# Sixteen expert blocks computed at the end of the first stage instead of at the start of the second

## The chip, the cores and the metric

One core of one Trainium2 chip runs the whole program. The core has TensorE (PE, with its weight loads shown apart as PEld), VectorE (DVE), ScalarE (ACT), GpSimd (POOL) and SyncE (SP, which here only issues DMAs). The metric is the device time in microseconds (us) of one execution; shown is the median of several runs. All engines take their instructions in order, each from its own queue, and wait for each other by semaphores.

## The reference

The input x has 32 sequences of 56 rows of 256 numbers; ctx has 32 x 1500 rows of 256. All is float32. Four layers follow each other, each with a residual:

```
x = x + xattn0(layernorm(x), ctx)   # decayed sum over ctx, projected, one vector per sequence; layernorm
x = x + ffn0(layernorm(x))          # 16 experts of width 176, the best 6 of each row
x = x + xattn1(layernorm(x), ctx)   # masked softmax attention over the 1500 rows
x = x + ffn1(layernorm(x))          # 2 experts of width 1024, the best one of each row

# ffn0, h: (1792, 256)
scores = softmax(h @ gate_w.T); topk_w, topk_idx = top_k(scores, 6)
y = sum over e of  cw[:, e] * ((silu(h @ w_gate[e].T) * (h @ w_up[e].T)) @ w_down[e].T)
```

Here only ffn0 matters, and the stage ahead of it that decides which rows go to which expert.

## The kernel before, in words

**Stages.** The kernel has four stages: a loop over 16 pairs of sequences (the first stage: context sum, first residual, normalised rows, choice of experts, sorting), the blocks of ffn0 (the second stage), attention, and the blocks of ffn1. Constants: P = 128, NP = 16 pairs, E0 = 16 experts, K0 = 6, F0 = 176, H0 = 88, NB0 = 95 blocks.

**First stage (lines 643 to 767).** Each step p of the loop streams two sequences' context through `ring`, five slots of SBUF (`count_in`, L315), and works at the same time on the pairs before: `first_norm`, `residual`, `second_root`, `second_norm` (L491, the normalised rows xn), `away` (L497, xn to the DRAM table `xn0`), `turned` and `gate` (the gating product), `best` (L511, the six best experts of each row, `sel`), `ranks` (L528, how many rows of each expert lie before), `counted` and `places` (L534, L540, each row's place in its expert's list and its level, that is the block of 128 in the list), `ones_at` (L566, one-hot rows, some experts' on DVE and some on POOL) and `sorted_in` (L588, matmuls that add to `owned` in PSUM: for each expert, level and place the row's number and its weight). `base0` counts the rows of each expert so far. In the last steps the weights of ffn0 are loaded into `w0_sb` (`load_w0_up`, L209; `w0_down_pieces`, L217, issued by `some_pieces`).

**The tail (lines 685 to 767).** After the loop come the last pair's steps, one after the other: norm, gate, `best(last)`, `ranks(last)`, `counted(last)`; then the table of blocks is made from the counts (`real`, `slot`, `blk`, `hot`), `owned` is copied out (L746), and eight matmuls (L750) turn it into `idx` (for each of the 95 blocks the numbers of its 128 rows), `wgt` (their weights) and `ei` (the place of the block's expert in `w0_sb`). Blocks are ordered by level: blocks 0 to 15 are the first 128 rows of the 16 experts, if each has any row. `busy(n)` (L579) runs n filler matmuls on PE.

**Second stage (`expert_blocks`, L769).** For each block: `rows_of` (L941) gathers its 128 rows from `xn0` by an indirect DMA on POOL's queue, seven blocks ahead; PE turns them (L195) and ACT copies them (L197); `gate_up` (L778) multiplies by gate and up weights (L785), ACT applies Silu (L791), DVE multiplies (L797); PE turns the product (L803), DVE copies it (L805), `down` multiplies (L812), ACT copies the result (L951) and SP writes it to the DRAM table `ys0` (L952). PE runs gate of block t, turn of t-1, rows of t+1 and down of t-2 in one step t. `side(t)` (L1039) does other work in each step: `ways_` (where each row's six results lie), windows of the context for the attention (`load_window`, one per step from step 1 to 16), a copy of xr to DRAM (step 17), mask rows, zero rows, and from step 20 on gathers of results (`result`, L853, POOL) that DVE adds to the rows (L1032).

**What sets the order.** Under `manual_schedule` an engine's instructions stay in the order in which the program writes them; this holds for PE, DVE, ACT and SP in the whole kernel, and for POOL too from the second stage on. In the first stage POOL's order is chosen by the framework's scheduler. SP issues transfers in program order. ACT needs its table of functions exchanged between logarithm/exponential and Silu. If `bad` is set at the end (some assumption on the data doesn't hold), a general path computes everything from ffn0 on again.

Of the kernel before, what the change touches and what calls it, by code (L numbers as in the profile page):

```python
# [19 lines left out]
P = 128  # L20
# [23 lines left out]
NB0 = NBW - E0 // 4  # L44
NY1 = 3
NB1 = B * S // P + 1
WP = 2 * D + 2
# [12 lines left out]
def xattn_ffn_kernel(  # L60
# [91 lines left out]
    starts = const.tile([1, B], I32, name="starts")  # L152
    bad = const.tile([1, 1], I32, name="bad")

    ring = const.tile([P, NRING, CW], F32, name="ring")
# [52 lines left out]

    def load_w0_up():  # L209
        for m, w in ((0, wg0), (1, wu0)):  # L210
            for k in range(KD):
                nc.sync.dma_start(
                    out=w0_sb[:, :, (2 * k + m) * F0 : (2 * k + m + 1) * F0],
                    in_=w[:, k, :].rearrange("p (e f) -> p e f", f=F0),
                )
# [18 lines left out]
    with tc.tile_pool(name="p1", bufs=1) as p1, tc.tile_pool(name="p3", bufs=3) as p3, tc.tile_pool(  # L234
# [151 lines left out]
        for l in range(NL):  # L386
            G.memset(lev[:, l, :], float(l * P))
        iota = p1.tile([P, P], F32, name="iota")
# [107 lines left out]
        def away(p):  # L496
            nc.sync.dma_start(out=xn0[p * P : (p + 1) * P, :], in_=pend[p]["xn"])  # L497
# [80 lines left out]

        def busy(n):  # L579

            for _ in range(n):
                d = psa.tile([P, 512], F32, tag="acc", name="d")
                PE.matmul(
                    d, lhsT=ident, rhs=slots[B % NRING][:, 0:2, :].rearrange("p j d -> p (j d)"),
                    start=True, stop=True,
                )

        def sorted_in(p, h=None):  # L588

            t = pend[p]  # L590
            for e in range(E0) if h is None else range(NE * h, NE * h + NE):
                c, g = divmod(e, 4)
                PE.matmul(  # L593
                    owned[Q * g : Q * g + Q, c, :],
                    lhsT=vals[:, p % 2, e].rearrange("p o l -> p (o l)"),
                    rhs=t["hots"][e // NE][:, e % NE, :],
                    start=(p == 0 and c == 0), stop=(p == NP - 1 and c == 3),
                )
# [42 lines left out]


        for p in range(NP):
            if p >= 1:
                first_norm(p - 1)
# [9 lines left out]
            if p >= 2:  # L655
                ranks(p - 2)
            sum_in_columns(p)
            if p >= 3:
                ones_at(p - 3, 1)
            if p >= 1:  # L660
                second_norm(p - 1)
                away(p - 1)
                some_pieces(1)
            projected(p)
            if p >= 3:
                sorted_in(p - 3)
            if p >= 1:
                turned(p - 1)
# [12 lines left out]
            if p == NP - 3:  # L681
                load_w0_up()
            if p > NP - 3:
                some_pieces(6)
        last = NP - 1
        first_norm(last)
        ones_at(NP - 3, 0)
        residual(last)
        ones_at(NP - 3, 1)
        second_root(last)  # L690
        ranks(NP - 2)
        second_norm(last)
        away(last)
        some_pieces(len(pieces))
        sorted_in(NP - 3, 0)
        turned(last)
        sorted_in(NP - 3, 1)
        gate(last)
        busy(1)
        counted(NP - 2)  # L700
        places(NP - 2)
        best(last)
        ranks(last)
        for h in range(2):
            ones_at(NP - 2, h)
        for h in range(2):
            sorted_in(NP - 2, h)
        counted(last)


# [14 lines left out]
        for c in range(4):  # L725
# [4 lines left out]
            )  # L730
        busy(1)
        places(last)
        for h in range(2):
            ones_at(last, h)
        blk = p2.tile([P, 4], F32, name="blk")
        V.tensor_copy(blk, bp[:, 0:4])
        hot = slots[B % NRING].rearrange("p j d -> p (j d)")
        own, hot = hot[:, 0 : 4 * P].rearrange("p (c r) -> p c r", c=4), hot[:, 4 * P :]
        hot = hot[:, 0 : 8 * NB0].rearrange("p (c b) -> p c b", c=4)
        V.tensor_tensor(  # L740
            hot, i99.rearrange("p o b -> p (o b)").unsqueeze(1).to_broadcast([P, 4, 2 * NB0]),
            blk.unsqueeze(2).to_broadcast([P, 4, 2 * NB0]), ALU.is_equal,
        )
        for h in range(2):
            sorted_in(last, h)
        A.copy(own.rearrange("p c r -> p (c r)"), owned.rearrange("p c r -> p (c r)"))  # L746
        bl = ps.tile([P, 512], F32, tag="ps", name="bl")
# [15 lines left out]
        PE.transpose(ep[0:1, 0:P], ex, ident)  # L763
        busy(2)
        V.tensor_copy(idx, bl[:, 0:NB0])
        V.tensor_copy(wgt, bl[:, P : P + NB0])
        V.tensor_copy(ei, ep[0:1, 0:P])

    def expert_blocks(nb, nq, f, w, ei, wk, ptr, pgu, pht, py, rows_of, done, ahead, wgt=None, side=None, xT0=None):  # L769

# [3 lines left out]
        piece = doff + 2 * D  # L774
        units = [(i, u) for i in range(nb) for u in range(nq)]
        xT, at, hs, hT, y = {}, {}, {}, {}, {}
# [42 lines left out]

        xb = {i: rows_of(i) for i in range(min(ahead, nb))}  # L820
        xT[0] = xT0 or turned_rows(wk, ptr, "tr", xb[0])
        xb.pop(0)
        if side:
            side(-1)
        for t in range(len(units) + 2):
            if t < len(units):
                gate_up(*units[t])
            if 0 <= t - 1 < len(units):
                turn(*units[t - 1])
            if t < len(units) and units[t][1] == nq // 2 and units[t][0] + 1 < nb:  # L830
                i = units[t][0] + 1
                if i + ahead - 1 < nb:
                    xb[i + ahead - 1] = rows_of(i + ahead - 1)
                xT[i] = turned_rows(wk, ptr, "tr", xb.pop(i))
            if t >= 2:
                down(*units[t - 2])
            if side:
                side(t)

# [88 lines left out]
    with tc.manual_schedule(  # L928
# [8 lines left out]
        zrow = rt.tile([P, WP], F32, name="zrow")  # L937
        G.memset(zrow, 0.0)
        G.memset(zrow[:, WP - 1 : WP], float(FAR))

# [70 lines left out]
        def late_or_bad():  # L1011
# [7 lines left out]
            V.tensor_reduce(t8s[0:1, 0, 0:1], lp[0:1, 0:P], AX.X, ALU.max)  # L1019
            V.tensor_scalar(bad, t8s[0:1, 0, 0:1], 0.0, bad, ALU.is_gt, ALU.max)  # L1020
            V.tensor_scalar(
                bad, slot[0:1, NL - 1, E0 - 1 : E0], float(NB0), bad, ALU.is_gt, ALU.max
            )

        todo = [(blocks_by(p) + 4, p, k) for p in soon for k in range(K0)]
        sums = []
# [12 lines left out]
        def side(t):  # L1039
# [5 lines left out]
            if t > 1:  # L1045
                for _ in range(3):
                    if ways_:
                        next_ = ways_.pop(0)
                        next_()
            if 0 < t <= B // 2:  # L1050
                load_window(t - 1)
            if t == B // 2 + 1:
                nc.sync.dma_start(
                    out=xr0.rearrange("(p r) d -> r p d", r=P), in_=xr,
                )
            if 0 < t - B // 2 - 1 <= B:
                b = t - B // 2 - 2
# [33 lines left out]
            NB0, 1, F0, w0_sb.rearrange("p e w -> p (e w)"), ei,  # L1091
            wk, ptr, pgu, pht, py, rows_of, done, 7, wgt, side,
        )
# [590 lines left out]
```

## Time and profile before

| | us |
|---|---|
| median of 7 runs | 781.97 |
| lowest, highest | 778.65, 783.93 |
| the profiled execution | 783.53 |
| its span (first to last instruction) | 781.8 |
| PE busy in the span | 672.3 |
| DVE busy | 402.0 |
| POOL busy | 351.3 |
| ACT busy | 238.0 |
| mean granted clock of PE | 0.945 of full |

The profile is of one execution. Its durations are those of single instructions; "idle before" is the time in which an engine waited ahead of an instruction, and what follows the arrow is what released it. A granted clock below 1 means that PE ran slower than it could. The DMA share is the mean busy share of 16 DMA engines and can read slightly above 1.

### The profile page before, as it was taken

What the parts mean: (1) busy time and instruction counts of PE and PEld (TensorE: products, weight loads), DVE (VectorE), ACT (ScalarE), POOL (GpSimd) and SP (SyncE); (2) the same over time, 40 slices, a digit from 0 to 9 for tenths busy, and PEclk for the clock granted to TensorE, in tenths of its full rate; (3) what the DMA queues carried; (4) which work ended last, traced back from release to release, by engine and by line L of the source; (5) the groups of instructions that cost most, each with busy time, mean ns of one, the idle gap of its engine ahead of it and who ended that gap; (6) DMA issues with size and microseconds to landing.
All of it is one profiled execution on the core that took longest, in us unless ns stands there. A gap on an engine that the chain in (4) does not pass through costs nothing.

```text
span 781.8 us, 13508 instructions
## 1 busy us (share of the span) xinstructions
PE 672.3 (86%) x4099; PEld 442.6 (57%) x4099; DVE 402.0 (51%) x1378; ACT 238.0 (30%) x704; POOL 351.3 (45%) x440
## 2 busy tenths in 40 slices
PE   3468878887789988788899888899987999999996
PEld 3334545554557766566566656556653566666664
DVE  3568787788436535333344334668787332333232
ACT  0123333333124433233333323266653111111110
POOL 5355566643243465366665665546642411221210
PEclk9779999997689999899999999999999899999999
DMA  8959999998248976344444443377881200110100
GB/s 264 365 225 376 351 370 366 340 344 258 65 132 265 309 255 201 87 131 133 123 133 125 123 140 112 108 233 202 220 272 51 95 13 22 41 27 28 41 28 17
DMA packets 70656, 136.62 MB, mean 175 GB/s; under 512 B 7731, under 2 KB 43204, under 8 KB 70580
## 3 DMA queue, kind: packets, MB, share of 16 engines
q1 hardware_dynamic: 56036, 100.31, 37.4%
q0 software_dynamic: 14544, 35.37, 16.4%
q8 instruction: 38, 0.62, 0.3%
q14 instruction: 38, 0.31, 0.1%
HBM read 109.54 MB, written 26.77 MB: 174 GB/s over the span
## 4 chain that ended last, share of the span: by engine, by line
PE 76%; DVE 8%; ACT 4%; issue 3%; POOL 3%; DMA 2%; another core or an unknown queue 1%; SPq 1%; POOLq 0%; DVEq 0%; ACTq 0%
PE gu L785 28%; PE y L812 18%; PE acc L325 6%; PE tp L803 4%; PE tp L195 4%; PE tp L913 2%; DMA xr<-in_x 2%; PE op L1177 2%; PE sp L1142 2%; ACT xT L197 2%; PE bp L467 1%; PE owned L593 1%; POOL xn L491 1%; PE lp L505 1%
## 5 line engine op out<-in xcount | busy, mean ns | idle before, releaser
L785 PE MATMUL gu<-w_sb,xT 128*128 x380 | 137.9, 486 | 29.2 <-ACT xT L197 22.1
L943 POOL DMA_INDIRECT xb<-xn,idx x95 | 93.1, 980 | 100.1 <-PE tp L195 51.2
L791 ACT ACTIVATE sg<-gu 128x176 f32<-128x176 f32 (+1 forms) x155 | 53.1, 343 | 252.5 <-PE gu L785 218.3
L797 DVE SCALAR_TENSOR_TENSOR hs<-sg,wgt,gu 128x176 f32<-128x176 f32 x95 | 37.8, 397 | 153.5 <-ACT sg L791 130.3
L785 PE MATMUL gu<-ring,xT 128*128 x240 | 114.7, 601 | 0.5 <-issue 0.5
L785 PEld LDWEIGHTS gu<-w_sb,xT 128*128 128x128 f32 x380 | 71.7, 197 | 65.5 <-ACT xT L197 29.7
L812 PE MATMUL y<-w_sb,hT 88*128 x380 | 99.7, 385 | 0.8 <-ACT yb L951 0.8
L856 POOL DMA_INDIRECT g<-ys,early x78 | 74.2, 951 | 36.0 <-issue 16.8
L795 DVE TENSOR_TENSOR hs<-sg,gu 128x256 f32<-128x256 f32 x60 | 25.2, 420 | 114.2 <-ACT sg L791 112.6
L803 PEld LDWEIGHTS tp<-ident,hs 128*88 128x88 f32 (+1 forms) x310 | 40.7, 132 | 62.4 <-issue 50.8
L1428 POOL DMA_INDIRECT out<-ob,ti x15 | 14.8, 989 | 130.2 <-DVE ob L1425 129.9
L812 PEld LDWEIGHTS y<-w_sb,hT 88*128 88x128 f32 x380 | 65.7, 193 | 6.8 <-ACT yb L951 1.0
L805 DVE COPY hT<-tp 88x256 f32<-88x256 f32 (+1 forms) x155 | 64.4, 416 | 8.1 <-PE y L812 5.0
L197 ACT COPY xT<-tp 128x256 f32<-128x256 f32 x126 | 46.9, 372 | 62.7 <-PE tp L195 38.7
L785 PEld LDWEIGHTS gu<-ring,xT 128*128 128x128 f32 x240 | 45.8, 192 | 33.5 <-issue 30.7
L812 PE MATMUL y<-ring,hT 128*128 x240 | 62.6, 384 | 0.0
L803 PE MATMUL tp<-ident,hs 128*88 128x128 f32 (+1 forms) x310 | 60.8, 279 | 1.7 <-issue 1.5
L325 PE MATMUL acc<-ring,cz 128*32 128x256 f32 x768 | 55.4, 447 | 0.3 <-DVE cz L301 0.3
L951 ACT COPY yb<-y 128x256 f32<-128x256 f32 x95 | 35.6, 375 | 55.0 <-PE y L812 34.2
L432 POOL TENSOR_SCALAR z<-xr,mva,rsa 128x256 f32<-128x256 f32 x16 | 23.0, 1437 | 49.2 <-DVE xr L479 45.0
L195 PE MATMUL tp<-ident,xb 128*128 128x128 f32 x220 | 43.1, 279 | 0.8 <-issue 0.8
L812 PEld LDWEIGHTS y<-ring,hT 128*128 128x128 f32 x240 | 41.5, 193 | 3.4
(307 smaller groups left out, 997.7 us busy)
## 6 DMA issues: line engine op xcount, KB each, us to landing
ring<-in_cx SPq DMA_DIRECT2D x32, 1536.0 KB
ys<-yb SPq DMA_DIRECT2D x95, 128.0 KB
ring<-in_cx SPq DMA_DIRECT2D x16, 384.0 KB
extra<-in_cx SPq DMA_DIRECT2D x16, 384.0 KB
xs<-zrow SPq DMA_DIRECT2D x5, 771.0 KB
w_sb<-in_wg SPq DMA_DIRECT2D x2, 1408.0 KB
w_sb<-in_wu SPq DMA_DIRECT2D x2, 1408.0 KB
xn<-xn SPq DMA_DIRECT2D x16, 128.0 KB
```

The source lines that it names most:

```text
L195: PE.transpose(tp[:, k * P : (k + 1) * P], xn[:, k * P : (k + 1) * P], ident)
L197: A.copy(xT.rearrange("p k c -> p (k c)"), tp[:, 0 : KD * P])
L325: PE.matmul(acc[Q * g : Q * g + Q, 0:D], lhsT=cz[:, j, 1 - h : 1 - h + Q], rhs=c[:, j, :], start=(h == 0 and m == 0), stop=(h == 1 and m = ...
L785: PE.matmul(gu[:, 0 : 2 * fp], lhsT=xT[i][:, k, :], rhs=w[:, bass.ds(at[i] + (u * piece + k * 2 * fp), 2 * fp)], start=(k == 0), stop=(k = ...
L791: A.activation(sg, gu[:, 0:fp], AF.Silu)
L797: V.scalar_tensor_tensor(hs[i, u], sg, wgt[:, i : i + 1], up, ALU.mult, ALU.mult)
L803: PE.transpose(tp[0:h, c * P : (c + 1) * P], a[:, c * h : (c + 1) * h], ident)
L805: V.tensor_copy(hT[i, u], tp[0:h, 0 : 2 * P])
L812: PE.matmul(y[i][:, 0:D], lhsT=a[:, c * P : (c + 1) * P], rhs=w[0:h, bass.ds(at[i] + (u * piece + doff + c * D), D)], start=(u == 0 and c ...
L856: G.indirect_dma_start(out=g, out_offset=None, in_=ys0[0 : n * P, :], in_offset=bass.IndirectOffsetOnAxis(ap=at[:, p, k : k + 1], axis=0),)
L943: G.indirect_dma_start(out=xb, out_offset=None, in_=xn0, in_offset=bass.IndirectOffsetOnAxis(ap=idx[:, i : i + 1], axis=0),)
L951: A.copy(yb, y[:, 0:D])
```

## The change

The first 128 rows of each expert are taken from the first eight pairs alone. What `owned` holds after pair 7 is copied out (`first_copy`, in step 10), and level 0 of it gives the rows and weights of blocks 0 to 15 (`first_table`, in step 11: `idx0`, `wgt0`). Their gathers (`soon_rows`) and their matmuls (`soon_turned`, `soon_gate`, `soon_step`) stand in program order among the last pair's steps, and what is left of them after `idx` is there. They use the slots of `ring` that the context no longer needs, the PSUM pools of the first stage, and constant addresses of `w0_sb`. `sorted_in` starts `owned` anew at pair 8, and the saved part is added at the end (DVE in place of ACT's copy). `lack` sets `bad` if an expert had fewer than 128 rows by pair 7 and got more later. The second stage starts at block 16: `expert_blocks` gets `first`, windows are loaded two per step from step 16 to 23, the copy of xr comes in step 15, gathers of results no earlier than step 24. POOL is in fixed order from step 15 of the first stage on. `busy` is gone. Silu now is needed first in the tail, after `best(last)`, so that the function table changes there, once. `load_w0_up` is split by experts: 0 to 3 and 4 to 11 in step 13, 12 to 15 at the end of step 15, followed by all the pieces that are left.

The core of the diff:

```diff
+PC = 8
-            G.memset(lev[:, l, :], float(l * P))
+            G.memset(lev[:, l, :], float(l * P) if l else -1.0)
...
+        def first_copy():
+            V.tensor_scalar(cut, base0[0:1, :], float(P), None, ALU.min)
+            A.copy(own0, owned.rearrange("p c r -> p (c r)"))
...
+        def soon_rows(n):
+            for _ in range(n):
+                i = len(egot)
+                if i < E0:
+                    egot.append(i)
+                    G.indirect_dma_start(
+                        out=xbs[i], out_offset=None, in_=xn0[0 : PC * P, :],
+                        in_offset=bass.IndirectOffsetOnAxis(ap=idx0[:, i : i + 1], axis=0),
+                    )
...
+        def soon_turned(i):
+            tp = ps.tile([P, 512], F32, tag="ps", name="tp")
+            for k in range(KD):
+                PE.transpose(tp[:, k * P : (k + 1) * P], xbs[i][:, k * P : (k + 1) * P], ident)
+            exT[i] = two_of("xT", 0, D).rearrange("p (k c) -> p k c", k=KD)
+            A.copy(exT[i].rearrange("p k c -> p (k c)"), tp[:, 0:D])
...
+        def soon_step(copy=A.copy):
+            t = eat[0]
+            eat[0] += 1
+            if t < E0:
+                gu = egu.pop(t)
+                sg = two_of("sg", 2 * D, F0)
+                A.activation(sg, gu[:, 0:F0], AF.Silu)
+                hs = two_of("hs", 2 * D + F0, F0)
+                V.scalar_tensor_tensor(
+                    hs, sg, wgt0[:, t : t + 1], gu[:, F0 : 2 * F0], ALU.mult, ALU.mult
+                )
+                if 2 <= t + 1 < E0:
+                    soon_gate(t + 1)
+                tp = ps.tile([P, 512], F32, tag="ps", name="tp")
+                for c in range(2):
+                    PE.transpose(tp[0:H0, c * P : (c + 1) * P], hs[:, c * H0 : (c + 1) * H0], ident)
+                ehT[t] = two_of("hT", D, D)[0:H0]
+                copy(ehT[t], tp[0:H0, 0 : 2 * P])
+            if t + 2 < E0:
+                soon_turned(t + 2)
+            if t >= 1:
...
+                yb = ybs[i % 8]
+                A.copy(yb, y[:, 0:D])
+                nc.sync.dma_start(out=ys0[i * P : (i + 1) * P, :], in_=yb)
...
         for p in range(NP):
+            if p == NP - 1:
+                pool_too.enter_context(
+                    tc.manual_schedule(engines={ET.PE, ET.DVE, ET.Activation, ET.SP, ET.Pool})
+                )
...
                 away(p - 1)
+                if p == NP - 1:
+                    soon_rows(2)
...
             if p == NP - 3:
-                load_w0_up()
+                load_w0_up(0, 4)
+                load_w0_up(4, 12)
             if p > NP - 3:
                 some_pieces(6)
+            if p == NP - 1:
+                A.copy(own.rearrange("p c r -> p (c r)"), own0)
+                load_w0_up(12, E0)
+                some_pieces(len(pieces))
         last = NP - 1
+        soon_turned(0)
+        soon_turned(1)
+        soon_rows(1)
         first_norm(last)
         ones_at(NP - 3, 0)
         residual(last)
         ones_at(NP - 3, 1)
+        soon_rows(2)
         second_root(last)
         ranks(NP - 2)
+        soon_gate(0)
         second_norm(last)
         away(last)
-        some_pieces(len(pieces))
+        soon_rows(2)
         sorted_in(NP - 3, 0)
         turned(last)
         sorted_in(NP - 3, 1)
         gate(last)
-        busy(1)
+        soon_gate(1)
         counted(NP - 2)
         places(NP - 2)
         best(last)
+        soon_rows(3)
         ranks(last)
+        soon_step()
         for h in range(2):
             ones_at(NP - 2, h)
+        soon_rows(2)
+        soon_step()
         for h in range(2):
             sorted_in(NP - 2, h)
         counted(last)
...
-        busy(1)
+        soon_step()
+        soon_rows(4)
         places(last)
         for h in range(2):
             ones_at(last, h)
+            soon_step()
...
+        soon_step()
         for h in range(2):
             sorted_in(last, h)
-        A.copy(own.rearrange("p c r -> p (c r)"), owned.rearrange("p c r -> p (c r)"))
+        V.tensor_tensor(own, owned, own, ALU.add)
+        soon_step()
...
-        busy(2)
         V.tensor_copy(idx, bl[:, 0:NB0])
         V.tensor_copy(wgt, bl[:, P : P + NB0])
         V.tensor_copy(ei, ep[0:1, 0:P])
+        while eat[0] < E0 + 1:
+            soon_step(V.tensor_copy)
...
-            if 0 < t <= B // 2:
-                load_window(t - 1)
-            if t == B // 2 + 1:
+            if t == E0 - 1:
+                G.memset(zrow, 0.0)
+                G.memset(zrow[:, WP - 1 : WP], float(FAR))
                 nc.sync.dma_start(
                     out=xr0.rearrange("(p r) d -> r p d", r=P), in_=xr,
                 )
+            if 0 <= t - E0 < B // 4:
+                for h in range(2):
+                    load_window(2 * (t - E0) + h)
```

## The prediction

> **What bounds the kernel now.** I read the busy time by stretch first, then the timeline around the end of the first stage and the first steps of the second, then the waits there. Columns of the first view: stretch, its length, busy time of PE, PEld, DVE, ACT and POOL (with counts), granted clock, DMA share, GB/s.
>
> ```profile
> 176.00:185.00 9.00, 7.87 (x102) 4.82 (x101) 7.48 (x29) 3.25 (x12) 4.13 (x7) 1.00 1.14 337
> 185.00:213.60 28.60, 20.48 (x146) 13.45 (x146) 17.71 (x54) 5.30 (x16) 7.20 (x11) 0.64 0.38 108
> 213.60:260.00 46.40, 43.12 (x188) 30.95 (x189) 22.12 (x73) 16.92 (x47) 20.17 (x22) 0.93 0.69 204
> ```
>
> The loop over pairs ends near 185.0. From there to the first expert matmul at 213.6, the tail, a DVE chain (places, one-hots, block table) sets the pace; PE is busy 20.48 us of 28.6, but at a clock of 0.64. From 213.6 on PE sets it (43.12 of 46.4). So PE time is scarce behind 213.6 and partly free before. One step of the second stage in its steady state:
>
> ```profile
> 228.81 1.35 PE L785 MATMUL gu<-w_sb,xT 128*128 x4
> 229.01 0.37 ACT L951 COPY yb<-y 128x256 f32<-128x256 f32 x1 [0.44 <-PE y L812]
> 229.99 0.38 PE L803 MATMUL tp<-ident,hs 128*88 128x128 f32 x2
> 230.21 0.38 PE L195 MATMUL tp<-ident,xb 128*128 128x128 f32 x2
> 230.43 1.03 PE L812 MATMUL y<-w_sb,hT 88*128 x4
> ...
> 231.29 1.05 PE L785 MATMUL gu<-w_sb,xT 128*128 x3
> ```
>
> From start to start: gate 1.18, turn of hs 0.22, turn of rows 0.22, down 0.86, together 2.48 us a block.
>
> **What is removed.** Blocks 0 to 15 leave the second stage. Their Silus (L791) start at 215.61 for block 0 and
>
> ```profile
> 260.04 0.32 ACT L791 ACTIVATE sg<-gu 128x176 f32<-128x176 f32 x1 [0.81 <-PE gu L785]
> ```
>
> for block 16: 44.4 us, which is 16 x 2.48 = 39.7 and a pause of 4.7 early on. These are the stage's cheap blocks: they carry no gathers of results (L856); the later 78 Silu intervals (260.04 to 507.02) average 3.17. The eight filler matmuls (L583, 6.58 us busy in the tail) go too.
>
> **What is added to the tail.** Sixteen blocks, 39.7 us of PE at full clock. The tail's own PE work is (20.48 - 6.58) x 0.64 = 8.9 at full clock, so of its 28.6 us 19.7 are free. Filled without a gap, the tail grows by 39.7 - 19.7 = 20.0. It won't be; I walk the queues in program order with the rows' durations and find three losses.
>
> - Front, 10.5. On DVE nothing is put ahead of the last choice (sel, ready at 194.3 now). But PE gets two turns and a gate ahead of its own last gate, 1.62 us, at the tail's clock 2.5, of which 1.2 fit its idle time: choice near 195.6. Then on ACT the exponential (0.5), the table load (1.28, the row at 213.00, so far hidden by the first gate) and a Silu (0.32), on DVE 0.40; the first turn of hs comes near 199. Turn of rows, its copy (0.37), gate 2, two turns and the first down at the low clock bring the sort of pair 14 (now 195.73) to 205.0. In those 20.0 us lie 9.5 of full-clock work.
> - Each step's wait, 5.1. In soon_step the Silu of block t stands on ACT behind the copy of block t-2's result, and the turn of hs behind one gate only: from the end of the down, 0.2 + 0.375 + 0.32 + 0.40 and four hand-overs of 0.03 to 0.24 make about 1.57, against a gate of 1.18. That is 0.39 in some 11 steps, plus 0.8 once, where places' scaling (0.51) stands ahead of a Silu.
> - Hand-over, 2.6: the last block has no gate to cover its hs (1.6), the first row block of the second stage none to cover its copy (1.0).
>
> So the tail grows by 20.0 + 10.5 + 5.1 + 2.6 = 38.2, its first gate of the second stage comes at 251.8, and 44.4 - 38.2 = **6.2** are saved, less what follows.
>
> **A pause behind dense gathers.** Eleven indirect loads leave POOL every 1.25 us from 209.03; then everything stands:
>
> ```profile
> 221.74 0.95 POOL L943 DMA_INDIRECT xb<-xn,idx  x1 [0.30 <-issue]
> ...
> 224.11 0.37 ACT L197 COPY xT<-tp 128x256 f32<-128x256 f32 x1 [2.88 <-remote]
> 224.29 0.94 POOL L943 DMA_INDIRECT xb<-xn,idx  x1 [1.61 <-remote]
> ...
> 224.54 2.72 PE L785 MATMUL gu<-w_sb,xT 128*128 x4 [2.36 <-issue]
> ```
>
> PE lost 2.36, then ran a gate at 2.72 instead of 1.45. While gathers come one per step (228 to 266) this doesn't recur. Now sixteen of them leave POOL near 183 to 205, and eleven more when the block table is there. Bounds: no pause, or three at 2.4 + 1.3 = 3.7 (11.1). I take one of 2.4, as most of the tail's gathers fall where PE waits anyway. Net gain: 6.2 - 2.4 = **3.8 us**.
>
> **Edits at nothing.** The early table (eight matmuls, four small copies in steps 10 and 11) lies under the stream of the context, whose DMA share is 0.93 from 45 to 165. The fixed order on POOL: in step 15 the four one-hots of pair 12 (2.4) precede the norm of pair 14 as now; those of pair 13 come after three gathers instead of at 183.14, ready near 189, read by PE after 192; those of pair 14 after ten gathers, near 200, read at 205. Without that cover, 2.4 each. On SP the last up-weights (four transfers) and the down pieces now precede the last away, which already leaves at 195.43; its rows are needed only once idx is there, then near 225. The gathers for blocks 16 on start there, under the last early steps, so that the 3 us from idx to the first turn are hidden.
>
> **Unknown sizes.** Landing of the early rows: 1.9 us from the end of issue at 210.14 to the turn at 212.04, but at 183 the DMA share is 1.14; the longest transfers queued there show 10.36 for two. Walked with 8 us instead of 2 the tail is 6 longer; I take 2 to 3, as 128 KB lie nearer to the first row. The 16 window loads come two per step over steps 16 to 23, on top of the copy of xr: between nothing (seven row blocks are ahead, 17 us) and the 3.7 that block 22 lost (interval 6.19) at a DMA share of 1.06. I take nothing. Clock: with PE warm throughout the walk ends 2 us earlier, with 0.95 throughout 2 later.
>
> **Two rules against rows.** PE stands from 186.2 to 187.8 and then takes 1.08 for 16 sorting matmuls that take 1.46 per 32 in the loop, so gaps of 1.6 already cost clock here. The Trainium skill ("TensorE: Matmul & The Clock Gate", What's actually happening) says that about 3.4 us of idleness lower the clock and as much sustained work restores it; by the page the front, whose gaps are 1 to 2 us, would stay warm, and the saving be 2 us larger.
> The gather at 285.81 took 1.29 instead of 0.95, beside a DVE addition of two SBUF tiles (L1032). The Trainium skill ("SBUF — State Buffer", Who interferes with whom) says that a vector instruction with two SBUF inputs holds off a GpSimd instruction that reads SBUF for its whole length, which speaks against gathers among DVE's one-hots: by the page three one-hots of 1.19 could each hold POOL, an estimate of 3.6 us later at worst.
>
> **Rivals.**
> 1. *The front fills.* If PE warms early and rows are there, 3 instead of 10.5 are lost and no pause shows: 3.8 + 7.5 + 2.4 = 13.7 gained. For it: DVE leaves ACT and PE idle there. Against: the table load and the choice are still in one chain.
> 2. *Slower: pauses of the gather bursts.* At three pauses of 3.7 instead of one of 2.4: 3.8 + 2.4 - 11.1 = 4.9 lost. It decides from the second full pause on (3.8 + 2.4 - 7.4 = -1.2). For it: 27 gathers in two bursts against 11 in one, and the later blocks at 3.17, where POOL again issues two per step. Against: the first burst falls into PE's idle time.
> 3. *Rows land late.* 6 us lost on landing: 2.2 slower.
> 4. *It doesn't do what it says*: an expert with fewer than 128 rows among the first eight pairs would send the kernel into its general path, hundreds of us. Eight pairs give at most 896 rows x 6 / 16 = 336 on average; under 1%.
>
> **Numbers.** The profiled execution took 783.53 (span 781.8), 1.56 above the median of 781.97. Forecast there 779.7; at the median 781.97 - 3.8 = **778.2**. Rival 1: 768.3. Rival 2: 786.9. Rival 3: 784.2. Chances: forecast 0.40 (its spread of some 5 us either way: faster 0.25, same 0.10, slower 0.05), rival 1 0.22, rival 2 0.22, rival 3 0.15 (same 0.05, slower 0.10), general path 0.01. Leaving 0.1 out on each side, the range goes from rival 1 to beyond rival 2 with a late landing in part: 768 to 790. The 0.3% (2.4 us) is about what a measurement of this kernel can tell from no change. Faster 0.47, same 0.15, slower 0.38.
>
> **What would show it.** Right: the first gate of the second stage near 252 to 255, block table near 225, early steps 2.9 us apart; clock in the tail above 0.9 from about 204; sort of pair 14 near 205; 79 blocks afterwards as now, some 250 us. Wrong: gaps of over 2 us marked remote in the tail (rival 2), the first turn of early rows later than 188 (rival 3), the first gate before 245 (rival 1), or more than 3.3 us per block in steps 16 to 36 with a DMA share of 1 (the windows).

## The result, and the profile after

| | before | after |
|---|---|---|
| median, us | 781.4 (46 runs, 775.82 to 789.0) | 798.08 (19 runs, 793.95 to 804.88) |
| the profiled execution, us | 783.53 | 794.07 |
| its span, us | 781.8 | 792.4 |
| mean granted clock | 0.945 | 0.938 |

The ratio is 1.0223 (95% interval 1.0205 to 1.0242): the change made the kernel 2.2% slower, and the time lies outside the range of 768 to 790. The profiled execution of after is among the fastest of its runs, so the traces show 10.5 us of the 16.7 between the medians.

The busy time by stretch of after, from the loop's end to the first gate of the second stage and the 46.4 us behind it (columns as in the prediction):

```profile
185.00:264.69 79.69, 64.08 (x364) 42.89 (x363) 31.19 (x95) 24.55 (x75) 31.38 (x36) 0.83 0.37 110
264.69:311.09 46.40, 42.05 (x194) 29.98 (x194) 25.51 (x84) 15.64 (x46) 26.14 (x27) 1.00 0.93 311
```

The tail is 79.69 long instead of 28.60, and PE stands for 15.6 us of it. The first gate comes at 264.69, not at 251.8. Block 16 in the timeline of after:

```profile
266.18 0.32 ACT L919 ACTIVATE sg<-gu 128x176 f32<-128x176 f32 x1 [1.68 <-PE gu L913]
```

That is 6.14 behind the 260.04 of before. The last block's Silu comes at 516.91, 9.89 behind, and the end 10.6 behind. Where the tail runs, it runs as forecast or better. Two early steps, timeline of after on PE and ACT:

```profile
239.66 1.35 PE L642 MATMUL gu<-w_sb,ring 128*128 128x352 f32 x4
239.86 0.37 ACT L680 COPY ring<-y 128x256 f32<-128x256 f32 x1 [0.44 <-PE y L675]
...
242.34 1.35 PE L642 MATMUL gu<-w_sb,ring 128*128 128x352 f32 x4
```

From gate to gate 2.68 (2.87 had been walked: 2.48 and 0.39). But three times it stands for several us (shorter stops follow later). The first time is in the front:

```profile
198.78 0.62 PE L509 MATMUL lp<-gw_sb,xT 128*128 128x16 f32 x4 [1.51 <-ACT xT L201]
199.94 0.95 POOL L624 DMA_INDIRECT ring<-xn,idx  x1 [0.30 <-issue]
...
203.45 0.17 ACT L518 COPY lg<-lp 128x16 f32<-128x16 f32 x1 [4.31 <-remote]
```

The last gating product is recorded as begun at 198.78 and 0.62 long; ACT copies it only at 203.45, and the profile finds no record on this core that ended when the wait did ("remote"). POOL has issued seven gathers in a row by then, from 193.19 to 202.1. The second time, behind eight gathers from 235.72 to 245.95 with a fill of 0.64 among them:

```profile
243.21 0.95 POOL L1069 DMA_INDIRECT xb<-xn,idx  x1 [0.30 <-issue]
...
245.00 0.95 POOL L1069 DMA_INDIRECT xb<-xn,idx  x1
247.23 0.42 DVE L666 COPY ring<-tp 88x256 f32<-88x256 f32 x1 [3.26 <-remote]
247.33 0.37 ACT L636 COPY ring<-tp 128x256 f32<-128x256 f32 x1 [3.79 <-remote]
...
247.75 2.72 PE L642 MATMUL gu<-w_sb,ring 128*128 128x352 f32 x4 [2.16 <-ACT ring L636]
```

DVE and ACT wait together for turns that PE has on record at 244.12 and 244.34; the next gate takes 2.72 instead of 1.35. The third and longest is in the second stage. POOL waits 14.23 for written results and then issues fifteen gathers without a gap:

```profile
333.13 0.94 POOL L984 DMA_INDIRECT g<-ys,early  x1 [14.23 <-DMA ys<-yb]
334.38 0.95 POOL L1069 DMA_INDIRECT xb<-xn,idx  x1 [0.30 <-issue]
...
347.41 0.32 ACT L919 ACTIVATE sg<-gu 128x176 f32<-128x176 f32 x1 [7.18 <-remote]
...
352.37 0.42 DVE L933 COPY hT<-tp 88x256 f32<-88x256 f32 x1 [4.21 <-remote]
354.58 0.37 ACT L201 COPY xT<-tp 128x256 f32<-128x256 f32 x1 [6.85 <-remote]
...
355.00 2.72 PE L913 MATMUL gu<-w_sb,xT 128*128 x4 [12.69 <-ACT xT L201]
```

PE stands for 12.69; the Silus of the two blocks concerned come 10.04 and 10.35 behind the ones before them, instead of 2.49.

What comes late in these stops is PE's word that its results are there. The trace also records the signals (semaphore events) by which the engines release each other, and each of the waits marked "remote" above ends 0.02 or 0.03 us behind a signal of PE: at 203.42 in the first stop; at 247.21, 247.25 and 247.31 in the second, for work whose last matmuls are recorded as begun at 244.24, 244.45 and 245.21; at 347.39, 352.35 and 354.56 in the third. "Remote" only says that PE's matmul had long been recorded as ended. DVE and ACT wait for PE's results. POOL goes on while its gathers need nothing of PE: in the third stop it issues them 1.25 apart up to 350.62, and only then waits, 3.19, for PE too. The stop of before that the prediction shows is of the same kind: ACT's wait to 224.11 ends with PE's signal at 224.03. So the prediction's "everything stands" says too much.

### The profile page after: what moved, and what is told of

The parts are those of the page before. It is cut to its first block, busy times and chain, and to the rows that moved or that the text cites. A ratio compares the mean times of both kernels' runs of the same rounds, so it can differ in the third digit from the quotient of the medians.

```text
span 792.4 us, 13412 instructions
## 1 busy us (share of the span) xinstructions
PE 673.5 (85%) x4107; PEld 440.9 (56%) x4107; DVE 401.7 (51%) x1378; ACT 238.6 (30%) x712; POOL 352.2 (44%) x440
## 4 chain that ended last, share of the span: by engine, by line
PE 74%; DVE 9%; ACT 4%; another core or an unknown queue 3%; issue 3%; POOL 3%; DMA 2%; SPq 2%; POOLq 0%; DVEq 0%; ACTq 0%
PE gu L913 25%; PE y L940 15%; PE acc L329 6%; PE tp L931 4%; PE tp L199 3%; PE gu L642 3%; PE tp L1041 2%; PE sp L1273 2%; PE y L675 2%; DMA xr<-in_x 2%; ACT xT L201 2%; PE op L1308 2%; PE owned L688 1%; PE bp L471 1%
## 5 line engine op out<-in xcount | busy, mean ns | idle before, releaser
L913 PE MATMUL gu<-w_sb,xT 128*128 x316 | 112.3, 478 | 36.2 <-ACT xT L201 28.5
L1069 POOL DMA_INDIRECT xb<-xn,idx x79 | 77.1, 976 | 106.9 <-PE tp L199 40.1
L913 PEld LDWEIGHTS gu<-w_sb,xT 128*128 128x128 f32 x316 | 58.0, 192 | 65.9 <-ACT xT L201 35.7
L925 DVE SCALAR_TENSOR_TENSOR hs<-sg,wgt,gu 128x176 f32<-128x176 f32 x79 | 31.4, 397 | 116.6 <-ACT sg L919 92.5
L940 PE MATMUL y<-w_sb,hT 88*128 x316 | 83.9, 389 | 1.2 <-DVE hT L933 1.2
L933 DVE COPY hT<-tp 88x256 f32<-88x256 f32 (+1 forms) x139 | 57.8, 416 | 7.5 <-remote 4.5
L940 PEld LDWEIGHTS y<-w_sb,hT 88*128 88x128 f32 x316 | 55.5, 196 | 6.5 <-issue 1.0
L201 ACT COPY xT<-tp 128x256 f32<-128x256 f32 x110 | 40.9, 372 | 49.6 <-PE tp L199 23.0
L931 PE MATMUL tp<-ident,hs 128*88 128x128 f32 (+1 forms) x278 | 53.9, 276 | 0.3 <-DVE hs L925 0.3
L329 PEld LDWEIGHTS acc<-ring,cz 128*32 128x32 f32 x768 | 27.8, 126 | 25.6 <-issue 13.7
```

The costliest lines, as they stand in the source:

```text
L201: A.copy(xT.rearrange("p k c -> p (k c)"), tp[:, 0 : KD * P])
L329: PE.matmul(acc[Q * g : Q * g + Q, 0:D], lhsT=cz[:, j, 1 - h : 1 - h + Q], rhs=c[:, j, :], start=(h == 0 and m == 0), stop=(h == 1 and m = ...
L913: PE.matmul(gu[:, 0 : 2 * fp], lhsT=xT[i][:, k, :], rhs=w[:, bass.ds(at[i] + (u * piece + k * 2 * fp), 2 * fp)], start=(k == 0), stop=(k = ...
L925: V.scalar_tensor_tensor(hs[i, u], sg, wgt[:, i : i + 1], up, ALU.mult, ALU.mult)
L931: PE.transpose(tp[0:h, c * P : (c + 1) * P], a[:, c * h : (c + 1) * h], ident)
L933: V.tensor_copy(hT[i, u], tp[0:h, 0 : 2 * P])
```

## The experiments

**Theory A**: PE stops behind dense runs of POOL's gathers, and the change makes more and denser runs (rival 2 of the prediction). **Theory B**: the order in the tail costs the time, by ACT's queue in the front, by a buffer shared with the sort of pair 14, or by two windows per step, and would do so anywhere.

### The change and the kernel before, unaltered

> The changed kernel itself once more, to have it beside the others on one chip. The chip of the four runs before this took 731.93 us for the kernel before (not 781.4) and showed no stop marked remote, and every block of the second stage took 2.49 us there. Theory A (the loss comes from stops of PE under dense gathers, which depend on the chip): on a chip without stops the changed kernel is within 1% of the kernel before, between 0.99 and 1.005 of it; on a chip with stops 1.015 to 1.03. Theory B (the loss is in the order of the tail, the same everywhere): 1.015 or more on any chip.

> The kernel before, for a profile on the same chip. Theory A: if its time is near 732, no stop marked remote and blocks with gathers of results at 2.49 to 2.8 us; if near 781, stops of 2 to 8 us as in the first profile. Theory B says nothing on it.

> The change unaltered, beside the others on the same chip. Theory A: ratio 0.994 to 0.998 where the kernel before takes about 732 us, 1.015 to 1.025 where it takes about 781. Rival (the sign hangs on something else than the chip): a ratio above 1.01 at 732 us.

> The change unaltered, beside front_roots_first_2 on the same chip. Theory A: ratio 0.994 to 0.998 where the kernel before takes about 732 us, 1.015 to 1.025 where it takes about 781.

The kernel before took 731.78 to 732.72 (medians) on the three chips of the experiments, not 781. (On which chip the result was taken is not on record.) The change took 729.56, 729.73 and 729.38: ratios 0.9956 (0.9929 to 0.9983), 0.9958 (0.994 to 0.9977) and 0.9964 (0.9944 to 0.9984). **There it is 0.4% faster, by 2.4 to 3.2 us.** (Two of the three chips ran it.) No profile of these runs, of either kernel, shows a stop marked remote. The same place as the first stop above, in the change without stops (control_after):

```profile
196.43 0.62 PE L509 MATMUL lp<-gw_sb,xT 128*128 128x16 f32 x4
...
197.25 0.15 ACT L518 COPY lg<-lp 128x16 f32<-128x16 f32 x1
```

0.82 from the product to its copy, where the other took 4.67. And the same place as the third: POOL catches up here too, with 20 gathers from 310.76 on, about 1.25 apart, and PE goes on in steps of 2.49.

```profile
310.76 0.94 POOL L984 DMA_INDIRECT g<-ys,early  x1 [9.23 <-DVE st L992]
...
334.60 0.95 POOL L1069 DMA_INDIRECT xb<-xn,idx  x1 [0.30 <-issue]
```

```profile
319.42 1.35 PE L913 MATMUL gu<-w_sb,xT 128*128 x4
...
321.91 1.35 PE L913 MATMUL gu<-w_sb,xT 128*128 x4
```

So the profiled executions with stops are longer by 783.53 - 733.08 = 50.5 us for the kernel before and by 794.07 - 730.77 = 63.3 for the change: 12.9 more, which turns a gain of 2.3 into the loss of 10.5. Theory B, which should hold anywhere, falls as the cause of the loss.

The two profiles with stops differ from all others in one more thing: part of the signals is missing in them. Before has 7275 of them on record where base_profile, the same kernel, has 10979; after has 7259 where control_after has 11081, and no other profile has fewer than 10979. Up to 185 us the counts agree (2118 and 2115; 2165 and 2169). From 185 to 600, where the gathers and the stops are, they are 4069 against 7929 and 3905 against 7976.

### The order on ACT

```diff
-        soon_turned(0)
-        soon_turned(1)
         soon_rows(1)
...
         ranks(NP - 2)
+        soon_turned(0)
+        soon_turned(1)
```

> The changed kernel, but the turns of the first two early row blocks stand behind second_root(last) and ranks instead of ahead of first_norm(last). In the changed kernel ACT copies these two blocks (191.59, 192.32) before it takes the root that the last pair's norm waits for (192.59; its input is there at 189.66). Theory A (order on ACT): the root comes within 0.3 us of its input, the last choice 2 to 3 us earlier, the time falls by 2 to 3 us. Theory B (PE sets the end of the tail anyway, the chain has room): less than 1 us.

> The change with the two early turns behind the last norm's root on PE and ACT. If the front's loss lies in the order on ACT (the copies of the first two turns ahead of the first root of the last pair), the last choice comes 0.8 us earlier and the stage's end 1 to 2 us: ratio to the kernel before 0.992 to 0.995 where control_after_3 has 0.995 to 0.997. Rival (the chain of sorts and steps sets the tail's end): no difference from control_after_3 beyond 0.001.

Ratios 0.9936 (0.9912 to 0.996) and, beside control_after_3, 1.0004 (0.9982 to 1.0025): no gain that repeats. From pair 14's choice to the last one it is 11.82 and 11.92 us instead of 10.23 and 10.16 (control_after, control_after_3), and to block 16 it is 64.95 and 65.05 against 66.67 and 64.98. The last choice comes no earlier, and the stage's start doesn't hang on it. (In w1_one_window, below, which has the front of the change, it takes 11.80 as well, so that the longer way is not clearly an effect of the order.)

### The table of blocks in a buffer of its own

```diff
+        at_own = slots[0].rearrange("p j d -> p (j d)")[0:1, 0 : 2 * E0 * NLP]
+        at_own = at_own.rearrange("p (e o l) -> p e o l", e=E0, o=2)
+        V.memset(at_own[:, :, :, NL:NLP], 0.0)
...
-        at_ = vals[:, NP % 2]
+        at_ = at_own
```

> The changed kernel, but the row of block numbers (at_) is written to a place of its own in the ring instead of over the values of pair 14, which the sort of pair 14 still reads. In the changed kernel DVE waits 4.28 us there (210.2 to 214.48) for matmuls that now stand behind two early steps. Theory A (this reuse is a link of the chain): the wait is gone, the last pair's places come some 4 us earlier, the table of blocks 2 to 4 us earlier, the time falls by 1 to 3 us. Theory B (PE is the bound from there on): places come earlier, the table and the time change by less than 1 us.

> The changed kernel with both the roots first on ACT and the row of block numbers in a place of its own. Both theories: 2 to 5 us less than the changed kernel on the same chip, as the two waits are in one chain (2.9 and 4.3 us in its profile) and PE is behind them.

`at_` lies in the buffer that the sort of pair 14 reads. Timeline of after, and of the kernel with a buffer of its own, on DVE:

```profile
214.48 0.53 DVE L842 SCALAR_TENSOR_TENSOR vals<-real,slot 1x224 f32<-1x224 f32 x1 [4.28 <-PE owned L688]
```

```profile
203.58 0.54 DVE L845 SCALAR_TENSOR_TENSOR ring<-real,slot 1x224 f32<-1x224 f32 x1
```

The wait is gone: counted from pair 14's choice, the table's input comes at 16.13 instead of 19.23 (control_after), block 16 at 63.88 instead of 66.67 (control_after_3: 19.17 and 64.98), so between 1.1 and 2.8 us of the 3.1 come through in the trace. The ratios, 0.9968 (0.9946 to 0.9991) and 0.9959 (0.9936 to 0.9981) together with the front's order, don't tell it from the change.

### The early rows loaded by SP

```diff
-                    G.indirect_dma_start(
-                        out=xbs[i], out_offset=None, in_=xn0[0 : PC * P, :],
-                        in_offset=bass.IndirectOffsetOnAxis(ap=idx0[:, i : i + 1], axis=0),
-                    )
+                    j = i % PC
+                    nc.sync.dma_start(out=xbs[i], in_=xn0[j * P : (j + 1) * P, :])
...
+            if p == NP - 1:
+                soon_rows(E0)
```

> The changed kernel, but the sixteen early row blocks are loaded by SP as whole blocks of the table, all at the start of step 15, instead of sixteen gathers on POOL; so the early blocks work on rows that aren't theirs. Theory A (bursts of gathers on POOL stop PE): the stop before the last choice (ACT waits 4.31 us for a product that PE issued at 198.78) is gone, the first turn doesn't wait for its rows, the last choice comes 5 to 7 us earlier and the time falls by 4 to 7 us. Theory B (that stop has another cause, such as fetching code): the stop remains, the time falls by at most 3 us, for the rows that are there earlier.

> The change with its sixteen early row blocks loaded by SP in plain transfers instead of gathered by POOL; the rows are the first ones of the normalised rows in storage order, not those the early table names, so this part of the computation is altered. Theory A: on a chip where the kernel before takes about 781 us, the tail loses its stop near 244 (about 4 us) and its POOL waits, the first gate of the second stage comes some 6 us earlier than in the change, and the ratio to the kernel before is near 1.013 instead of 1.022; on a chip at 732, ratio 0.997. Rival (order of the tail): first gate and ratio as in the change.

0.9969 (0.9947 to 0.999) and 0.9958 (0.9937 to 0.9979): as the change. Where nothing stops, sixteen gathers off POOL are worth nothing. Whether it saves a stop where there are stops could not be seen.

### Windows

> The changed kernel, but one window of the context per step (steps 16 to 31) instead of two (16 to 23). In the changed kernel's profile the writes of block results queue behind the windows, POOL's gather of results waits 14.23 us for them (to 333.13), then 15 gathers leave in a row and PE stands 12.69 us. Theory A (the windows start this): the wait on POOL falls to under 3 us, no stop of PE over 5 us between steps 16 and 50, the time falls by 7 to 12 us against the changed kernel (to about 787 to 791). Theory B (the loss lies in the tail alone, where early blocks and sort share in-order queues, and stops of PE in the second stage come either way): at most 2 us less (796 to 798).

> The change with the two early turns behind the last norm's root on PE and ACT, the context windows loaded one in two steps from step 24 on instead of two per step from step 16, and the mask product on POOL near the end of the stage. Theory A (PE is stopped behind dense runs of gathers where a chip shows stops; elsewhere the forecast's terms hold): at 732 us for the kernel before, POOL's wait of some 14 us for written result rows in steps 34 to 40 is gone, but it is hidden there by the seven row blocks ahead, so the gain is that of the early turns alone, ratio 0.992 to 0.996; at 781 us the stop of some 10 us at block 42 goes, ratio at most 1.008. Rival (windows and mask product cost time by themselves, through the DMA share): ratio below 0.990 at 732 us.

One window per step from step 16 on: 1.0007 (0.9976 to 1.0037). One in two steps from step 24 on, the mask product late, and the front's order as above: 0.9959 (0.9922 to 0.9996), with POOL's longest wait for written results down to 4.7. Spreading the windows brings nothing where nothing stops.

### Fewer rows ahead

```diff
-            wk, ptr, pgu, pht, py, rows_of, done, 7, wgt, side, None, E0,
+            wk, ptr, pgu, pht, py, rows_of, done, 4, wgt, side, None, E0,
```

with one window per step and the mask product late.

> The change, with its dense runs of row gathers thinned: 4 row blocks instead of 7 are gathered ahead when the block table is there, one context window per step is loaded instead of two, and the product of the mask rows on POOL is made near the end of the stage instead of in step 56, so that POOL does not stand for SP's backlog and catch up in a run. Theory A (PE is stopped behind dense runs of indirect gathers, on chips that show such stops at all): on a chip where the kernel before takes about 732 us, no difference from the change beyond 2 us, ratio to the kernel before 0.99 to 1.00; on a chip where it takes about 781, stops in steps 16 to 60 of the second stage shrink from 25 us or so to under 10, ratio below 1.005. Rival (the loss is in the order of the tail alone): ratio as the change on either chip, 1.02 where before takes 781.

A miss for both theories: 1.0105 (1.006 to 1.015), slower without any stop marked remote. POOL and PE in its timeline:

```profile
312.74 0.94 POOL L984 DMA_INDIRECT g<-ys,early  x1 [16.05 <-DMA ys<-yb]
```

```profile
317.20 0.66 PE L199 MATMUL tp<-ident,xb 128*128 128x128 f32 x2 [5.58 <-DMA xb<-xn,idx]
```

POOL stands 16.05 for written results; the rows of the blocks stand behind it in its queue, and four blocks ahead (10 us) don't cover that; seven (17.4) would. Here rows are really late, and PE waits *ahead* of the turn, with the transfer named; block 41 comes 12.62 behind block 40, 10.1 more than 2.49, which is about the whole difference to the change (1.0105 against 0.996, 10.6 us of 732). In the stops of after PE has its matmuls on record and those who read the result wait. They are two different things.

### More gathers in the kernel before

```diff
+            if t == 6:
+                for j in range(10):
+                    g = resp.tile([P, D], F32, tag="g", name="g")
+                    G.indirect_dma_start(
+                        out=g, out_offset=None, in_=xn0,
+                        in_offset=bass.IndirectOffsetOnAxis(ap=idx[:, 40 + j : 41 + j], axis=0),
+                    )
```

> The kernel before with ten more gathers in step 6 of the second stage, in one burst on POOL; nothing reads what they fetch. Seven row blocks are ahead (17 us), the burst takes 12.5 us. Theory A (bursts stop PE on a chip with stops): where the kernel before is near 781, a stop of PE of 3 to 8 us within 12 us of the burst's start and 3 to 8 us more time; where it is near 732, no stop and less than 1 us. Theory B (stops come from something else, such as fetching code): no stop there on any chip, less than 1.5 us.

> The kernel before with ten more row gathers in one run in step 6 of the second stage, whose rows nobody reads. Theory A: on a chip where the kernel before takes about 732 us, no stop, ratio 1.000; on a chip where it takes about 781, PE is stopped for 3 to 6 us within 10 us of the run, block 16 that much later, ratio 1.003 to 1.008. Rival: nothing stops on either chip, ratio 1.000.

> The kernel before with ten more row gathers in one run in step 6 of the second stage, whose rows nobody reads. Theory A: at 732 us for the kernel before no stop, ratio 1.000 to 1.002; at 781 us PE is stopped for 3 to 6 us within 10 us of the run, ratio 1.003 to 1.008. Rival: no stop at 781 us either.

> The kernel before with one more row gather per step in steps 4 to 19 of the second stage, whose rows nobody reads, so that POOL issues two per step there as it does later. Theory A: where the kernel before takes about 732 us no stop, blocks 2.49 us apart, ratio 0.998 to 1.003; where it takes about 781, stops of about 1 us every second block or fewer and larger ones, block 16 between 5 and 15 us later, ratio 1.006 to 1.02. Rival (density alone does not stop PE): blocks 2.49 apart and ratio 1.000 at 781 us too.

1.0006 (0.9984 to 1.0027), 1.0022 (1.0 to 1.0045), 0.9982 (0.9961 to 1.0002); with one more gather per step in steps 4 to 19, 1.002 (1.0001 to 1.0039). Blocks stay 2.49 apart while 21 gathers leave POOL in a row (burst_in_before, from 228.62). In these runs a dense run alone stops nobody. None of them met the stops, so that a run of gathers *causes* them was not tried; it rests on where they stand in the two traces. In before with stops, steps 5 to 20 have one gather per step and blocks 2.48 to 2.49 apart without exception, and the steps behind them, with two, lose 0.7 per block on average (0.1 in base_profile). In after, no step of the tail between 223 and 235, where POOL issues nothing, shows one: the gates there are 2.62, 3.72 and 4.46 apart, as in control_after.

## Why the prediction was wrong

**The failed step is the pause behind dense gathers** ("I take one of 2.4, as most of the tail's gathers fall where PE waits anyway"). Counted from pair 14's choice to the first gate of the second stage, the tail grew by 37.6 us without stops (control_after 65.18 against 27.59; control_after_3, with 63.49, by 35.9) and by 48.0 with them (76.26 against 28.27). The lines it is counted from: pair 14's choice in the timelines of before, base_profile, after and control_after on DVE, and the busy time by stretch from the first gate on in base_profile and control_after (that of before begins at 213.6, that of after at 264.69).

```profile
185.32 0.23 DVE L523 TENSOR_SCALAR sel<-rp,valid 128x16 f32<-128x16 f32 x1
185.67 0.24 DVE L523 TENSOR_SCALAR sel<-rp,valid 128x16 f32<-128x16 f32 x1
188.43 0.25 DVE L527 TENSOR_SCALAR sel<-rp,valid 128x16 f32<-128x16 f32 x1
187.91 0.26 DVE L527 TENSOR_SCALAR sel<-rp,valid 128x16 f32<-128x16 f32 x1
```

```profile
213.26:259.66 46.40, 45.47 (x205) 33.32 (x206) 24.32 (x80) 18.89 (x52) 21.38 (x24) 0.94 0.74 223
253.09:299.49 46.40, 45.48 (x216) 33.74 (x217) 29.80 (x107) 18.67 (x54) 29.05 (x31) 1.00 1.02 349
```

The 38.2 of the working was right to 0.6 and 2.3 us where nothing stops; the stops cost 10.4 to 12.1, not 2.4. The argument that the first run of gathers falls into PE's idle time failed: the stop of 4.3 stood on the last gating product, at the head of the chain of choice, sort and steps. Two stops make it: counted from pair 14's choice, the early gates are 6.9 behind those of control_after between the first stop and the second, and 10.9 behind the second. The working had also put the pause of 4.7 among the removed blocks down as saved. But the run of gathers for the first blocks of the second stage still stands in the change, eight of them from 235.72, and the second stop is at its end.

Rival 2 named the stops and the sign. That its price, three times 3.7 or 11.1, meets 10.4 to 12.1 is in part luck, as the tail had two larger ones; and its 786.9 was 11 us short of the 798.08.

**A run in the second stage was not seen.** The loss goes on behind the tail: block 16 to the last one took 250.7 against 247.0. The longest stop, 12.69, follows POOL's wait of 14.23 for written results and its catching up. "I take nothing" for the windows overlooked that SP's writes of results queue behind them and that POOL then catches up in one run; where nothing stops, the seven row blocks ahead do cover it, as the working said.

**The early table was not free.** The prediction laid it under the stream of the context. Timeline of after on PE:

```profile
146.43 0.38 PE L535 MATMUL rk<-sel,ones 128*128 128x16 f32 x2
146.66 1.93 PE L598 MATMUL bl<-ident,w_sb 128*128 128x4 f32 x16
148.44 0.59 PE L450 MATMUL sp<-sel,acc 128*128 128x2 f32 x4
```

The eight matmuls are 16 instructions, and the step's own chain waits behind them. From pair 9's choice to pair 10's every profile of the change has 11.15 us or more, where the kernel before has 9.2 to 9.7. Over the loop that is 1.6 to 2: 130.63 to 130.83 against 128.87 to 129.10 from the first choice to pair 14's, and 133.1 to 133.2 against 131.25 to 131.4 in executions with a slip of some 2 us near 90 us that both kernels show; four profiles of the change took 134.0 to 135.6 and one 137.8. That it is the table is read from where the delay stands; no run leaves the table out. Between the two profiles of the result the loop is 3.1 longer: 4.0 from the table and this slip, less a start that was 0.9 earlier.

**The sum.** Against the 779.7 forecast for the profiled execution: loop +3.1, tail 48.0 - 38.2 - 2.4 = +7.4, blocks 16 to the last +3.8, the rest +0.1: 794.07. Without stops: the removed blocks cost less too, since the pause of 4.7 in them isn't there (block 0 to block 16 is 40.3, not 44.4). The same working then gives about 2.1 saved in place of 6.2; measured were 1.75 at block 16 (254.58 against 256.33) and 2.3 at the end, out of 4.0 in the tail less 2.2 in the loop.

**By the list of signs.** Early steps came 2.49 to 2.69 apart where no other work of the tail and no stop lay between (2.9 predicted). The sort of pair 14 came at 213.26 and without stops at 205.91 (near 205). `idx` came at 234.64 and without stops at 227.23 (near 225). The first gate came at 264.69 and without stops at 253.09 (252 to 255). The first turn of early rows came at 190.89, later than 188 (rival 3's sign): 3.5 us from the end of its gather's issue where 2 to 3 were taken, on a loop that ended 3.1 later. The clock of the tail stayed low for longer than predicted (0.9 from 204): 0.60 from 205 to 215 and 0.83 from 215 to 225, 0.81 and 1.00 without stops. The sign of rival 2, gaps of over 2 us marked remote, was there. The 79 blocks took 250.7, near "some 250", but 203.5 without stops.

**The two rules.** The trace agrees with the row, not with the Trainium skill ("TensorE: Matmul & The Clock Gate", What's actually happening): in control_after PE stands 2.38 ahead of its first early turn at 189.97, and the gate at 192.03 takes 2.69 instead of 1.35; the clock is 0.67 from 185 to 195. And of the page "SBUF — State Buffer" (Who interferes with whom) little is seen: the sixteen early gathers took 0.94 to 1.32 in after, together 1.2 us over 0.95 each, not 3.6.

**What stays open.** Why PE's signals come late in a stop; whether it belongs to the chip or to something around it at that time; and whether fewer gathers in a row would end the stops. Two rivals have something on record. Fetching code, Theory B of some expectations, isn't seen: the profile lists the packets of the instruction queues, and none moved from 195 to 208 or from 240 to 260 in after, nor from 212 to 230 in before, which takes in the first two stops and the one that the prediction shows. The recording of the execution is untested: the signals are missing just where the stops are, and no run tells whether a common cause lies behind both, or whether the recording itself held PE up.

## What to carry to other kernels

A stop that one trace shows is a price of the place where it was measured: before a change makes more of what stands ahead of it, its cost should be taken once per such run, not once in all, and the time should be measured on more than one chip and occasion. A wait for which the profile names no releaser should be followed to the signal that ended it. The early table was not hidden by the loop's busy DMA share: its matmuls of 1.93 stand beside 1.6 to 2 us more in the loop. When a queue holds both urgent and patient gathers, the rows fetched ahead must cover the longest wait of the patient ones.

## What was not expected of the hardware

The same kernel took 781.4 in the runs of the result and 732 on the three chips of the experiments, with single durations that agree (0.95 per gather, 2.49 per block where nothing stops) and a mean granted clock of 0.945 and 0.955. The difference stands almost whole in the second stage's gather phase: its last 78 blocks take 247.0 with stops and 203.7 without. In a stop PE's results are signalled late, and ACT and DVE wait 2 to 7 us for them, while SP's and POOL's transfers go on moving (118 GB/s from 328 to 356 in after). In the runs without stops a stream of gathers 1.25 apart left the blocks 2.49 apart.
